# The conditional layer with its weights standing in the array and its result turned by DMA, and the last pair's base product undivided

## The chip, the cores and the metric

The kernel runs on one core of one Trainium2 chip. The metric is the device time of one execution in microseconds (us). A core has a matrix engine (PE, with its weight loads shown apart as PEld), a vector engine (DVE), a scalar engine (ACT), a pool engine (POOL) and a sync engine (SP) that issues most of the DMAs. Each engine works through its own queue in order: an instruction that waits holds everything behind it on that engine.

## What is computed

The input `x` is 64 samples of 64 channels by 1024 features. A block with a residual is followed by another one:

```python
y  = einsum('bct,bcd->bdt', x, cond_weights[itok_0_15])      # conditional layer: a 64 x 64 matrix for each sample
qkv = y.reshape(8, 8*64, 1024) ... @ qkvw + qkvb              # attention over 64 tokens, 32 heads of 32
x1 = x + softmax(q k / sqrt(32)) v @ ow + ob
base   = x1 @ W.T                                             # second conditional layer: base product and
logits = x1 @ Wr.T + language bias; top 2; softmax            #   two of eight low-rank experts
z  = bf16(base + 2 * sum(gate * (x1 @ A.T) @ B))
out = x1 + ffn(z)        # int8-like quantization, gate and up products, silu, clip, quantization, down product
```

All products but those of the feed-forward part are in float32, which the matrix engine takes in two instructions for each product of the program.

## The kernel before

**Stages.** The 4096 token rows are eight blocks of 512. `attention` (line 183) computes the conditional layer, q, k and v, scores, softmax and context, block by block. `OutProjection` (line 1069) multiplies by `ow` and adds the residual, for pairs of 256 rows. `second_stage` (line 1188) does the base product, the router, the experts and the feed-forward part, also by pairs. The large products (q, k, v, `ow`, `W`) are done as seven products of quarters (class `Winograd`, line 1009): with the token quarters `B11`, `B12`, `B21`, `B22` (features by tokens) and sums of them, `T1` to `T4`.

**The conditional layer.** A tile is two samples, 128 rows by 1024 features. `conditional` (line 342) copies the two 64 x 64 matrices of a tile into the diagonal of a 128 x 128 tile `wbd` (line 380), and multiplies eight 128 x 128 pieces of `x` as standing weights with `wbd` as moving data (line 355). So the result leaves the array already turned, features by tokens. Copies on DVE and ACT (lines 361, 363) put it into the token quarters `yB`, and four DVE instructions (line 376) form the sums `T`. This is eight pieces of work for each block; those of block b + 1 stand in the last phase of block b, ahead of its v and q, k products.

**The order in a block.** A block has four phases, c = 0 to 3 (`NP`), each for a quarter of the columns of q and k. During phase c the PE does the q and k products for c + 1 (`rows_job`, line 423); in phase 0 also the second half of v, in phase 3 the first half of v and the first q and k of the next block (`values_job`, line 456). In each phase two groups are begun (`group`, line 585), each with its score products (line 498, tile `s`), at the start and in the middle. When two groups have their probabilities turned, their context products (line 550, tile `c`) come right after the scores of a group. The order is planned by hand: `run` (line 615) adds up the costs that the author gave to the pieces in a clock `now`, and `at` files a step under the time when it is to be put into its engine's queue. A group's steps are: DVE takes the maximum and the difference, ACT the exponential (line 514), DVE normalizes, ACT parts the float32 numbers into two planes of 16-bit halves (line 528, tile `ph`, 6.8 planned us after the scores), SP turns them with a DMA transpose (line 533, tile `phT`), and 8 us later ACT joins the planes (line 540, tile `pT`).

**What a k job leaves.** The seven products come in the order 1, 6, 7, 5, 2, 4, 3. Product 2 is copied by four ACT instructions (line 419) into `kbd`, the block-diagonal keys, which have one buffer only; the others are added by DVE (line 421). The scores of the next phase read `kbd`, and so must wait for these copies.

**Loads.** `load_qk` (line 285) loads the seven combined quarters of q's or k's weights, 1792 KB, through SP at the end of the job that frees one of two buffers. In block 0 they are loaded raw and summed by the engines. `load_x` (line 239) loads the four tiles of the next block's `x`, 512 KB each, at the start of a block; POOL gathers the matrices `wg` by indirect DMA.

**The end.** The last pair p = 15 has an order written out by hand (lines 1554 to 1632), interleaved with the rest of pairs 14 (`q`) and 13 (`r`): `base` is one of seven products of four pieces, `after` its sums on DVE or ACT, `lora` the experts' product, `quant_a` and `quant_b` the quantization (by DVE and ACT) and the turning of its result (by DMA, or by the PE where the last argument is True), `gate_or_up`, `scaled`, `glu`, `down` and `result` the feed-forward part.

Of the kernel before, what the change touches and what calls it, by code (L numbers as in the profile page):

```python
# [11 lines left out]
F32 = mybir.dt.float32  # L12
# [170 lines left out]
def attention(tc, a, x_t, ctx_d, ident, dram, ps_g, KC, PB, NBLK, NCH, HPC, H, C, chores, early, op):  # L183
# [27 lines left out]
    with ExitStack() as ctx, ExitStack() as mid:  # L211
# [13 lines left out]
        w = pool(early, "w1", 1)  # L225
        xp = pool(early, "xp", 4)

# [10 lines left out]

        def load_x(b):
            tiles = []  # L240
            for j in range(PB):
                i = b * PB + j
                xt = xp.tile([P, H], F32, tag="x", name=f"x_{i}")
                if i == PB - 1:
                    held(xt[:, 0:1], tiles[0][0])
                nc.sync.dma_start(xt, x_t[i])
                wg = xp.tile([P, C], F32, tag="wg", name=f"wg_{i}")
                nc.gpsimd.indirect_dma_start(
                    out=wg[:, :],
                    out_offset=None,  # L250
                    in_=cw,
                    in_offset=bass.IndirectOffsetOnAxis(ap=idx[:, i:i + 1], axis=0),
                )
                tiles.append((xt, wg))
            return tiles

# [28 lines left out]
        def load_qk(b, wh, c, eng=None):  # L285
            t = w_qk[b, wh, c] = wp.tile([P, 7, KQ, P], F32, tag="wqk", name=f"w{wh}_{b}_{c}")
            if b == 0:
                if (wh, c) == ("q", 0):
                    held(t[:, SLOT["A11"], 0, 0:1], x_next[0][1])
                for key in RAW:  # L290
                    nc.sync.dma_start(t[:, SLOT[key], :, :], quarter(key, (0 if wh == "q" else H) + c * P, P))
                return sums(
                    eng or nc.vector, lambda key: t[:, SLOT[key], :, :], lambda: nc.gpsimd.dma_start(qk_d[wh, c], t)
                )
            nc.sync.dma_start(t, qk_d[wh, c])
# [20 lines left out]
        bqkv = act.tile([P, 3 * KC], F32, tag="bqkv", name="bqkv")  # L316
        x_next = load_x(0)
        first_sums = load_qk(0, "q", 0) + load_qk(0, "k", 0, nc.gpsimd)
# [5 lines left out]

        wbd = []
        for j in range(PB):
            t = w.tile([P, P], F32, tag=f"wbd{j}", name=f"wbd{j}")
            nc.vector.memset(t, 0.0)
            wbd.append(t)
        kbd, vbd = [], []  # L330
# [10 lines left out]

        def conditional(b, tiles):

            def one(hf, j):
# [3 lines left out]
                def product():  # L348
                    xt = tiles[j][0]
                    if j % 2 == 0:  # L350
                        B[key] = yp.tile([P, KQ, HB], F32, tag=key, name=f"y{key}_{b}")
                    ps = ps_g.tile([P, 4, P], F32, tag="g", name=f"cond_{b}_{j}_{hf}")
                    for q in range(KQ):
                        k = hf * KQ + q
                        nc.tensor.matmul(ps[:, q, :], xt[:, k * P:(k + 1) * P], wbd[j], start=True, stop=True)
                    box.append(ps)

                def rest():
                    dst = B[key][:, :, (j % 2) * P:(j % 2 + 1) * P]
                    if j % 2 == 0:  # L360
                        nc.vector.tensor_copy(dst, box[0])
                    else:
                        nc.scalar.copy(dst, box[0])  # L363
                    if (hf, j) == (0, 3):
                        t_of("T1", "B12", "B11")
                    elif (hf, j) == (1, 3):
                        t_of("T2", "B22", "T1")
                        t_of("T3", "B22", "B12")
                    elif (hf, j) == (1, 1):
                        B["T4"] = B["B12"]  # L370
                        nc.vector.tensor_tensor(B["T4"], B["B21"], B["T2"], ALU.subtract)
                return 0.95, product, rest

            def t_of(key, x, y):
                B[key] = yp.tile([P, KQ, HB], F32, tag=key, name=f"{key}_{b}")
                nc.vector.tensor_tensor(B[key], B[x], B[y], ALU.subtract)

            for j, (_, wg) in enumerate(tiles):
                for r in range(2):
                    (nc.gpsimd if b else nc.vector).tensor_copy(wbd[j][halves[r], halves[r]], wg[halves[r], :])  # L380
            return [one(0, j) for j in range(PB)] + [one(1, j) for j in (2, 3, 0, 1)]

# [197 lines left out]
        def contexts(least=1):  # L580
            ready = sum(len(pTs) == 2 for *_, pTs in waiting)
            for n in range(ready if ready >= least else 0):
                context(*waiting.pop(0), 1.7 * n * (least - 1))

        def group(b, c, us):


            def begin():
                ps = scores(b, c, us)
                if behind:  # L590
                    behind.pop()()
                contexts(2)
                pTs = []
# [85 lines left out]

        for f in conditional(0, x_next):  # L680
            run(*f)
# [4 lines left out]
        for f in qk_fill(0, 0) + v_fill(0, 0):  # L686
            run(*f)
        for b in range(NBLK):
            if b + 1 < NBLK:
                x_next = load_x(b + 1)  # L690
            for c in range(NP):
                fills, length = [], None
                if c + 1 < NP:
                    fills += qk_fill(b, c + 1)
                    if c == 0:
                        fills[7:7] = v_fill(b, 1)
                        if b == 0:
                            for at_ in range(3, 7):
                                with_sums(fills, at_, v_raw, 1)
                elif b + 1 < NBLK:  # L700

                    fills += conditional(b + 1, x_next) + v_fill(b + 1, 0) + qk_fill(b + 1, 0)
                else:
# [484 lines left out]
def second_stage(tc, a, out_t, xT_d, ident, ps_g, KC, NT, H, C, half, comb, op):  # L1188
# [12 lines left out]
    with ExitStack() as ctx:  # L1201
# [165 lines left out]
        def base(p, i):  # L1367
# [10 lines left out]
            elif i == 3:  # L1378
                lora(p, ps, 1, bmd)

        def lora_5(p):
            lora(p, st[p]["ps", 5], 1, bm[:, hs[1]])
# [22 lines left out]
        def quant_a(p, t, nm, between=None):  # L1405
# [11 lines left out]
            nc.vector.tensor_reduce(am, q, AX.X, ALU.max, apply_absolute_value=True)  # L1417
            sc = s["sc", nm, t] = sm.tile([P, 1], F32, tag="sc" + nm, name=f"sc_{nm}_{p}_{t}")
            nc.vector.tensor_scalar(sc, am, 1.0 / QMAX, 1e-8, ALU.mult, ALU.max)
# [52 lines left out]
        def down(p, t):  # L1472
            s = st[p]
            qT = s.pop(("qT", "i", t))
            for n in range(2):
                ps = s["pd", t, n] = ps_h.tile([P, HH], F32, tag="h", name=f"pd_{p}_{t}_{n}")
                for k in range(IC):
# [3 lines left out]

        def result(p, t, adds=None):
            s = st[p]
            y = p2.tile([P, H], F32, tag="y", name=f"y_{p}_{t}")
            si = s.pop(("sc", "i", t))
            for n in range(2):
# [3 lines left out]
                if adds:  # L1490
                    adds.tensor_add(y[:, hs[n]], y[:, hs[n]], s["x", t][:, hs[n]])
                    nc.sync.dma_start(out_t[2 * p + t, :, hs[n]], y[:, hs[n]])
# [10 lines left out]
        for p in range(NPAIR - 1):  # L1503
# [17 lines left out]
            do(old, quant_b, q, 0, "u")  # L1521
            base(p, 7)
            do(last, down, r, 1)
            do(last, result, r, 1)
# [40 lines left out]
        down(r, 0)  # L1565
        token_sums(p)
        quant_a(r, 1, "i")
        base(p, 1)
        after(p, 1)
        route(p)  # L1570
        quant_b(r, 1, "i")
        result(r, 0)
        base(p, 6)
        base(p, 7)
        gates_transposed(p)
        after(p, 6)
        quant_a(q, 0, "u")
        base(p, 2)
        after(p, 2)
        after(p, 7)  # L1580
        quant_a(q, 1, "g", (q, 0, "u"))
        down(r, 1)
        result(r, 1)
        quant_a(q, 1, "u", (q, 1, "g"))
        gate_or_up(q, 0, "g")
        scaled(q, 0, "g")
        base(p, 4)
        after(p, 4)
        gate_or_up(q, 0, "u")
        quant_a(p, 0, "g", (q, 1, "u"))  # L1590
        scaled(q, 0, "u")
        base(p, 5)
        lora_5(p)
        after(p, 5)
        quant_a(p, 0, "u", (p, 0, "g"))
        glu(q, 0)
        gate_or_up(q, 1, "g")
        quant_b(p, 0, "u")
        base(p, 3)
        scaled(q, 1, "g")  # L1600
        after(p, 3)
        gate_or_up(q, 1, "u")
        quant_a(p, 1, "g")
        gate_or_up(p, 0, "g")
        scaled(q, 1, "u")
        quant_a(p, 1, "u", (p, 1, "g"))
        gate_or_up(p, 0, "u")
        quant_a(q, 0, "i")
        glu(q, 1)
        quant_b(p, 1, "u", True)  # L1610
        gate_or_up(p, 1, "g")
        quant_a(q, 1, "i", (q, 0, "i"))
        gate_or_up(p, 1, "u")
        down(q, 0)
        scaled(p, 0, "g")
        scaled(p, 0, "u")
        quant_b(q, 1, "i")
        glu(p, 0)
        scaled(p, 1, "g")
        scaled(p, 1, "u")  # L1620
        result(q, 0)
        quant_a(p, 0, "i")
        down(q, 1)
        glu(p, 1)
        quant_b(p, 0, "i", True)
        result(q, 1, nc.gpsimd)
        quant_a(p, 1, "i")
        down(p, 0)
        result(p, 0, nc.gpsimd)
        quant_b(p, 1, "i", True)  # L1630
        down(p, 1)
# [55 lines left out]
```

## Time and profile before

| what | value |
|---|---|
| median of 3 runs | 2462.17 us (2460.88 to 2463.17) |
| the profiled execution's own time | 2461.01 us |
| its span in the profile | 2459.1 us |
| PE, DVE, ACT, POOL busy | 99%, 62%, 39%, 15% of the span |
| DMA queues q1 (SP), q0, q10 | 52.9%, 7.7%, 2.0% of 16 engines |
| granted PE clock | 0.995 of full |

The profile is of one execution, recorded by the hardware. Times are us from the start of the span, unless marked ns. A row of groups gives line, engine, operation, the tile written <- the tiles read, the shape, the count, then the busy time in us and the mean ns of one, and after the second bar the engine's idle time ahead of them with what ended it. A row of the timeline gives start, duration, engine, line and operation; in brackets the idle time before it and its releaser. A matmul's row shows two instructions for each float32 product, and the duration of each overlaps with the next: the distance from one row's start to the next one's is the time it takes. The DMA rows give the median us from issue to landing.

### The profile page before, as it was taken

Reading aid. Unit: us, or ns where it says so; the run is one execution under the profiler, and the core shown is the slowest. Engines: PE = TensorE matmul, PEld = TensorE weight load, DVE = VectorE, ACT = ScalarE, POOL = GpSimd, SP = SyncE. Lnnn points to the kernel's source line nnn. Section 1 sums busy time; section 2 is a strip of 40 time slices with the busy share of each in tenths; the row PEclk is TensorE's granted clock in tenths of the full one; section 3 lists DMA queues with packets and bytes.
Section 4 is the critical chain, followed back from the end, with each engine's and each line's share of the span. In section 5 each row is a group of like instructions: output and inputs, shape, how many; then the busy total and the mean of one; then the engine's idle time right before and its main releaser. Section 6 shows DMA issues by size and latency. Waiting matters only on the chain.

```text
span 2459.1 us, 34200 instructions
## 1 busy us (share of the span) xinstructions
PE 2423.2 (99%) x13194; PEld 1699.6 (69%) x13232; DVE 1533.1 (62%) x2957; ACT 952.8 (39%) x1303; POOL 363.4 (15%) x451
## 2 busy tenths in 40 slices
PE   8999999999999999999999999999999999999996
PEld 7888888888888888888888544444454545454452
DVE  4685585775664755745646623333367777778787
ACT  1353353342443533534424544344323333333333
POOL 5110001011122221210000233333200000000001
PEclk9999999999999999999999999999999999999998
DMA  8895767676677767775547588876744344434343
GB/s 280 284 264 152 219 200 238 188 208 210 201 198 250 206 194 246 207 208 175 177 137 234 170 258 255 263 243 215 242 126 83 84 79 88 80 81 87 70 95 72
DMA packets 417980, 446.76 MB, mean 182 GB/s; under 512 B 299665, under 2 KB 353938, under 8 KB 404114
## 3 DMA queue, kind: packets, MB, share of 16 engines
q1 hardware_dynamic: 387298, 377.90, 52.9%
q0 software_dynamic: 12080, 49.82, 7.7%
q10 hardware_dynamic: 18432, 16.79, 2.0%
q8 instruction: 106, 1.74, 0.3%
q14 instruction: 64, 0.52, 0.1%
HBM read 272.97 MB, written 100.66 MB: 152 GB/s over the span
## 4 chain that ended last, share of the span: by engine, by line
PE 94%; DVE 2%; ACT 2%; DMA 1%; issue 0%; ACTq 0%; SPq 0%; DVEq 0%
PE psva L462 5%; PE pska L435 5%; PE psvd L462 5%; PE psqa L435 5%; PE psvc L462 4%; PE pbc L1031 4%; PE pba L1031 4%; PE psqc L435 4%; PE pskc L435 4%; PE psqd L435 4%; PE pskd L435 4%; PE pbd L1031 4%; PE poa L1031 4%; PE pod L1031 4%; PE poc L1031 4%; PE s L498 3%
## 5 line engine op out<-in xcount | busy, mean ns | idle before, releaser
L540 ACT COPY pT<-phT 128x1024 int16<-128x1024 int16 x128 | 167.2, 1342 | 84.8 <-DMA phT<-ph 84.6
L514 ACT ACTIVATE prob<-prob 128x512 f32<-128x512 f32 x128 | 80.6, 630 | 259.4 <-DVE prob L511 232.1
L421 DVE SCALAR_TENSOR_TENSOR kbd<-pskd,bqkv,psku 32x256 f32<-32x256 f32 x256 | 123.1, 481 | 31.6 <-PE pskd L435 27.8
L528 ACT COPY ph<-prob 128x1024 int16<-128x1024 int16 x128 | 130.8, 1047 | 24.3 <-DVE prob L522 23.7
L1152 POOL TENSOR_TENSOR xo<-xo,ob 128x1024 f32<-128x1024 f32 x32 | 84.1, 2648 | 351.7 <-DVE To L1042 305.5
L561 ACT ACTIVATE co<-c,bqkv 128x256 f32<-128x256 f32 x128 | 60.1, 469 | 179.6 <-PE c L550 152.1
L435 PE MATMUL psqa<-yB,wq 128*128 128x256 f32 x512 | 123.6, 384 | 0.5 <-ACT psqp L406 0.5
L435 PE MATMUL pska<-yB,wk 128*128 128x256 f32 x512 | 122.6, 382 | 0.0
L1495 POOL DMA_DIRECT2D out_dram<-y x29 | 25.2, 869 | 652.3 <-DVE y L1487 652.3
L1126 ACT COPY xh<-xo 128x1024 int16<-128x1024 int16 x64 | 64.1, 1040 | 142.4 <-DVE xo L1171 142.4
L462 PE MATMUL psva<-wv,yB 128*128 128x256 f32 x512 | 117.0, 382 | 0.4
L1031 PE MATMUL poa<-woA,cx 128*128 128x512 f32 x256 | 115.4, 593 | 0.0
L1031 PE MATMUL pba<-wtA,x1T 128*128 128x512 f32 x256 | 115.1, 592 | 0.0
L1137 ACT COPY xTo<-xhT 128x1024 int16<-128x1024 int16 x64 | 84.7, 1339 | 58.4 <-DMA xhT<-xh 52.1
L435 PEld LDWEIGHTS pska<-yB,wk 128*128 128x128 f32 x512 | 96.0, 190 | 15.0 <-issue 2.6
L435 PEld LDWEIGHTS psqa<-yB,wq 128*128 128x128 f32 x512 | 95.2, 190 | 16.0 <-issue 2.8
L462 PEld LDWEIGHTS psva<-wv,yB 128*128 128x128 f32 x512 | 96.1, 190 | 14.1 <-ACT yB L363 1.0
L510 DVE TENSOR_REDUCE mx<-s 128x8 f32<-128x512 f32 x128 | 87.7, 685 | 10.7 <-PE s L498 9.3
L511 DVE TENSOR_TENSOR prob<-s,mx 128x512 f32<-128x512 f32 x128 | 88.5, 691 | 9.3 <-DVE mx L510 0.5
L522 DVE TENSOR_TENSOR prob<-prob,den 128x512 f32<-128x512 f32 x128 | 88.5, 692 | 4.4
L520 DVE TENSOR_REDUCE den<-prob 128x8 f32<-128x512 f32 x128 | 86.7, 678 | 7.2 <-ACT prob L514 6.3
L1031 PEld LDWEIGHTS poa<-woA,cx 128*128 128x128 f32 x256 | 48.4, 190 | 60.1 <-issue 59.9
(243 smaller groups left out, 5135.5 us busy)
## 6 DMA issues: line engine op xcount, KB each, us to landing
wv<-v_d SPq DMA_DIRECT2D x98, 512.0 KB, 3.9
wq<-q_d SPq DMA_DIRECT2D x28, 1792.0 KB, 7.7
wk<-k_d SPq DMA_DIRECT2D x28, 1792.0 KB, 8.1
x<-in_x_dram SPq DMA_DIRECT2D x32, 512.0 KB, 9.1
ctx_d<-co ACTq DMA_DIRECT2D x128, 128.0 KB, 4.2
cx<-ctx_d SPq DMA_DIRECT2D x16, 1024.0 KB, 6.9
xo<-in_x_dram SPq DMA_DIRECT2D x32, 512.0 KB, 5.7
xT_d<-xTo SPq DMA_DIRECT2D x64, 256.0 KB, 3.2
```

The lines of the kernel that those rows point to most:

```text
L421: nc.vector.scalar_tensor_tensor(dst, ps, bias, u, ALU.add, ALU.add)
L435: nc.tensor.matmul(ps[:, 0:HB], A[:, SLOT[A_OF[i]], k, :], B[B_OF[i]][:, k, :], start=first and k == 0, stop=k == KQ - 1, skip_group_check ...
L462: nc.tensor.matmul(ps[:, j * VC:(j + 1) * VC], B[B_OF[i]][:, k, j * P:(j + 1) * P], A[:, k, :], start=first and j == 0 and k == 0, stop=k ...
L510: nc.vector.tensor_reduce(mx_v, ps, AX.X, ALU.max)
L511: nc.vector.tensor_tensor(p.rearrange("p (a e) k -> p a e k", a=2), ps, mx_v.unsqueeze(3).to_broadcast([P, 2, HPC, C]), ALU.subtract)
L520: nc.vector.tensor_reduce(den, p, AX.X, ALU.add)
L522: nc.vector.tensor_tensor(p, p, den.unsqueeze(2).to_broadcast([P, n, C]), ALU.mult)
L528: nc.scalar.copy(h, planes(p.rearrange("p n k -> p (n k)")))
L540: nc.scalar.copy(planes(pT.rearrange("p a b q -> p (a b q)")), hT)
L1031: self.nc.tensor.matmul(ps, self.B[self.B_OF[i]][:, k, :], self.A[self.A_OF[i]][:, k, :], start=first and k == 0, stop=k == self.KQ - 1, s ...
L1137: nc.scalar.copy(planes(xT.rearrange("p k q -> p (k q)")), hT)
L1152: nc.gpsimd.tensor_add(s["x"][:, t, :], s["x"][:, t, :], self.ob)
```

## The change

The conditional layer of blocks 1 to 7 is turned round. `wg` itself stands in the array, in quarters of 64 x 64, and `x` moves: four products of 64 rows by 512 columns for a tile, one for each quarter of the array, into two tiles of the pool `ps_c`, which the context products use too. The result is tokens by features, so it is parted into 16-bit planes by ACT (`yh`, a pool with one buffer), turned by a DMA transpose through SP (`yhT`, two buffers) and joined by ACT into the token quarters, which now have two sets, for even and odd blocks. That is for each tile two transposes and five ACT instructions. The tiles stand singly in the order: at the start of those groups that have no context products, and once in phase 0 between jobs. The sums `T` of the next block stand in the last two products of phase 2 and the first two of phase 3. `x` has two buffers instead of four, and a tile's load is issued when the tile two before it has been multiplied. Block 0 keeps the old way, with its tiles lent from the quarters.

For the last pair the base product is not done in seven products but in four, one for each half of the tokens and half of the columns, of eight pieces each (`undivided`), with the raw quarter `A21` of the weights loaded for it in the iteration before. The sums of tokens and the sums after the products fall away, and the order of the last pairs is written anew.

```diff
-        xp = pool(early, "xp", 4)
+        xp = pool(early, "xp", 2)
...
-        wbd = []
-        for j in range(PB):
-            t = w.tile([P, P], F32, tag=f"wbd{j}", name=f"wbd{j}")
-            nc.vector.memset(t, 0.0)
-            wbd.append(t)
+        wbd = yp.tile([P, KC, P], F32, tag="B21", name="wbd")
+        nc.vector.memset(wbd, 0.0)
...
+        def conditional_tile(b, j):
+            xt, wg = x_of.pop((b, j))
+            ps = [ps_c.tile([P, 2, HB], F32, tag="c", name=f"cond{hf}_{b}_{j}") for hf in range(2)]
+            for hf in range(2):
+                for r in range(2):
+                    nc.tensor.matmul(
+                        ps[hf][halves[r ^ hf], :, :], wg[halves[r], :], xt[halves[r], hf * 512:(hf + 1) * 512],
+                        start=True, stop=True,
+                    )
+            if j + 2 < PB:
+                load_x(b, j + 2)
+            elif b + 1 < NBLK:
+                load_x(b + 1, j + 2 - PB)
+            def parted_y(hf):
+                h = w.tile([P, 2, 512], I16, tag="yh", name=f"yh_{b}_{j}_{hf}")
+                nc.scalar.copy(h, planes(ps[hf].rearrange("p a t -> p (a t)")))
+                at(now + 1.7, lambda: turned_y(hf, h))
+            def turned_y(hf, h):
+                hT = w.tile([P, 2, 512], I16, tag="yhT", name=f"yhT_{b}_{j}_{hf}", bufs=2)
+                nc.sync.dma_start(
+                    hT.rearrange("p h (k q) -> p (h k) q", q=P), h.rearrange("p h t -> p (h t)"), transpose=True
+                )
+                at(now + 5.1, lambda: joined_y(hf, hT))
+            def joined_y(hf, hT):
...
+                for r in range(2) if hf else (slice(0, P),):
...
+                    nc.scalar.copy(dst, src[:, :, :, halves[r] if hf else r])
+            at(now + 1.7, lambda: parted_y(0))
+            at(now + 5.1, lambda: parted_y(1))
...
-                contexts(2)
+                if not contexts(2) and (b, c, us[0]) != (0, 0, 0):
+                    next_tile()
...
+                        n = 7 if b else 14
+                        fills[n:n] = [(0.9, next_tile, None)]
+                    if c + 2 == NP and b + 1 < NBLK:
+                        sums_to_come = [lambda b=b, n=n, Y=Y: t_of(b + 1, Y, *T_OF[n]) for n in range(4)]
+                        with_sums(fills, -2, sums_to_come, 1)
+                        with_sums(fills, -1, sums_to_come, 1)
...
-                    fills += conditional(b + 1, x_next) + v_fill(b + 1, 0) + qk_fill(b + 1, 0)
+                    fills += v_fill(b + 1, 0) + qk_fill(b + 1, 0)
+                    with_sums(fills, 0, sums_to_come, 1)
+                    with_sums(fills, 1, sums_to_come, 1)
...
+        def undivided(p, t, n):
...
+            ps = s["ps", t, n] = ps_g.tile([P, HH], F32, tag="g", name=f"pb{t}{n}_{p}")
+            for h in range(2):
+                for k in range(KQ):
+                    nc.tensor.matmul(
+                        ps, s["xT"][:, t, h * KQ + k, :], AT[f"A{n + 1}{h + 1}"][:, k, :],
+                        start=(h == 0 and k == 0), stop=(h == 1 and k == KQ - 1), skip_group_check=True,
+                    )
+        def completed(p, t, n):
+            lora(p, st[p]["ps", t, n], t, bm[:, hs[n]])
+        def rounded(p, t, n):
+            s = st[p]
+            nc.scalar.copy(s["z"][:, t, hs[n]], s.pop(("ps", t, n)))
...
+            if p == NPAIR - 2:
+                AT["A21"] = wa.tile([P, KQ, HH], F32, tag="wtS3", name="wtA21")
+                nc.sync.dma_start(AT["A21"], quarters(a["w_t"])[:, 0, :, 1, :])
```

In the new order of the last pairs the four `undivided` products stand where the seven `base` products stood, a `quant_a` of 1024 columns is split in halves for the last tile (`quant_half`, `quant_whole`), the last `down` products use the pool `ps_g`, the quantized up input of the last tile is turned by DMA and no longer by the PE, and one of the two last additions to the result of tile 0 moves from POOL to DVE.

## The prediction

> **What bounds the kernel now.** I read the page first. These are its busy times and the row of the PE in 40 slices:
>
> ```profile
> PE 2423.2 (99%) x13194; PEld 1699.6 (69%) x13232; DVE 1533.1 (62%) x2957; ACT 952.8 (39%) x1303; POOL 363.4 (15%) x451
> PE   8999999999999999999999999999999999999996
> ```
>
> The PE is the bound everywhere but in the last slice. So an edit wins what PE time it takes out, and loses what PE wait it puts in. Next, the group of the old conditional products, and where they stand in one block (timeline of the PE):
>
> ```profile
> L355 PE MATMUL cond<-wbd,x 128*128 128x128 f32 x512 | 61.7, 282 | 10.2 <-DVE wbd L380 9.5 <-DVE yB L361 0.7
> ```
>
> ```profile
> 350.57 7.41 PE L355 MATMUL cond<-wbd,x 128*128 128x128 f32 x64
> 357.82 3.62 PE L462 MATMUL psva<-wv,yB 128*128 128x256 f32 x16
> ...
> 475.65 1.10 PE L498 MATMUL s<-kbd,qT 64*64 64x128 f32 x32
> 476.69 1.99 PE L435 MATMUL pska<-yB,wk 128*128 128x256 f32 x8
> ...
> 488.97 1.10 PE L498 MATMUL s<-kbd,qT 64*64 64x128 f32 x32
> ```
>
> Start to start, a block's conditional layer takes 7.25 us, a group's scores 1.04 us, and the second half of phase 1 (block 2) 13.32 us. ACT in that half:
>
> ```profile
> 478.35 0.63 ACT L514 ACTIVATE prob<-prob 128x512 f32<-128x512 f32 x1 [5.57 <-DVE prob L511]
> 479.74 0.63 ACT L514 ACTIVATE prob<-prob 128x512 f32<-128x512 f32 x1 [0.76 <-DVE prob L511]
> 480.27 0.35 ACT L406 COPY pskp<-pska 128x256 f32<-128x256 f32 x1
> 480.53 2.55 ACT L540 COPY pT<-phT 128x1024 int16<-128x1024 int16 x2
> 482.93 1.99 ACT L528 COPY ph<-prob 128x1024 int16<-128x1024 int16 x2
> 485.62 1.92 ACT L419 ACTIVATE kbd<-pska,bqkv 32x256 f32<-32x256 f32 x4 [0.70 <-PE pska L435]
> ```
>
> The last row is what counts: `kbd` is ready at 487.54, and the scores that read it start at 488.97. The slack is 1.43 us, although ACT is idle more than half of the time on average. Then the DMA issues of three short stretches: the start of block 1, a quiet stretch of phase 1, and the load of the q weights at 475.75.
>
> ```profile
> x<-in_x_dram SPq DMA_DIRECT2D x4, 512.0 KB, 9.1
> wk<-k_d SPq DMA_DIRECT2D x1, 1792.0 KB, 7.0
> ...
> phT<-ph SPq DMA_TRANSPOSE x2, 6.0
> ```
>
> ```profile
> phT<-ph SPq DMA_TRANSPOSE x2, 3.2
> ```
>
> ```profile
> wq<-q_d SPq DMA_DIRECT2D x1, 1792.0 KB, 9.4
> ```
>
> A transpose lands after 3.2 us in the quiet stretch, and after 6.0 where loads were issued on SP's queue ahead of it: what is issued later comes later. Last, the tail of the PE:
>
> ```profile
> 2429.48 1.03 PE L1439 MATMUL qTp_u<-ident_b,qb_u 128*128 128x128 bf16 x8 [7.18 <-DVE qb_u L1432]
> 2430.31 3.41 PE L1449 MATMUL pg<-wg,qT_g 128*128 128x512 bf16 x8
> 2433.55 1.89 PE L1449 MATMUL pu<-wu,qT_u 128*128 128x512 bf16 x8
> ```
>
> **Conditional products.** A new tile is four products of 64 rows and 512 columns, two instructions each. The nearest row is the scores: sixteen products of 128 columns on the same four quarters of the array in 1.04 us. Four of 512 move as many columns, so a tile costs 1.03, and a block 4 x 1.03 = 4.12. Saved: 7.25 - 4.12 = 3.13 us in each of seven blocks, 21.9, and 0.7 for the wait on `yB` in the group row. Here a rule speaks against the change. The Trainium skill (TensorEngine Tiling (Array Packing), Gotcha 1: PSUM Pressure) says that different row tiles must not use one PSUM bank at once. The scores keep to it (each half of the rows writes its own bank); a new tile does not, since both halves of the rows write into both banks. If the halves then take turns, a tile costs about 1.9 us, 28 tiles 53, and the gain of 22.6 is gone. I take the row, 1.03, as nothing shows that the two writes at different partitions collide, and keep 1.9 for the range.
>
> **What the tiles put on ACT and SP.** For each tile ACT gets two partings (row L528: 1.0 each), one joining of 1.3 (L540) and two halves of it at 0.7, 4.7 us in all, and SP two transposes. On average ACT has room. But the parting of the second half needs the one buffer `yh`, which is free only when the transpose of the first half has landed. That transpose is put in 1.7 planned us before the parting, and needs 3.0 us at the least (tile `phT`: 3.0/3.5/7.5 from issue to landing). So ACT stands still at each tile, and everything behind it on ACT with it: one `pT`, the partings of the probabilities, the first joining, and the copies to `kbd`, for which the next scores, hence the PE, wait.
>
> I walk through the half shown above, where tile 3 of the block stands. Times count from the start of its scores, S. PE: scores 1.03, tile 1.03, seven products 7 x 1.727; the next scores are due at S + 14.2. SP: the load of wq is issued at S + 0.1 and lands at S + 9.5, as before; behind it the `x` tile (512 KB; that stretch of block 1 moved 318 GB/s, so 1.6 us) and the first transpose (about 1.4 once it starts): it lands at S + 12. ACT: the exponentials, the first parting, the copy of product 1 and one `pT` are done at S + 7.3; then 4.7 us of standing still. From S + 12: parting 1.05, `pT` 1.27, two partings 2.0, joining 1.3, four copies to `kbd` 1.92, which gives S + 19.6. **The PE waits 5.4 us** at the scores of phase 2. Where tile 2 or tile 1 falls into a q or v job, nothing on the PE waits (next bank needed some 3 us later), though ACT is behind and costs 0.7 at the next block's start.
>
> Sum over blocks: 5 x 5.4 = 27 in blocks 1 to 5; 4.1 in block 6, which has no `x` to load; in block 0, where the tiles come one group later, 4.4 (tile 2, behind raw quarters of wq) and 2.4 (tile 1 in the k job, no load ahead): together 38; 0.7 at five starts, 3.5. In all 41.4. From both sides: if the transpose landed in its quiet 3.2 us, ACT's own work would just reach and the wait would be 0 to 0.3; if the load lasts 1 us longer, it is 6.4.
>
> The clock, too. After 7.18 idle us eight gate products took 3.24 us (2430.31 to 2433.55) and not 1.73. The Trainium skill (TensorE: Matmul & The Clock Gate, What's actually happening) lets the clock fall to half after an idle window of 3.4 us, windows running freely. By the trace's row alone (7.18 us) a wait of 5.4 may cost nothing or 1.5; by the rule it holds a whole window 6 times in 10. I take 0.7 for six blocks: 4.
>
> **Edits at nothing.** The removed copies on DVE (28 x 0.68) and POOL (56 x 0.28) lay under PE work. The sums `T` move into the k job of phase 2, where DVE is busy 11 of 13 us; each stands a product ahead of its use, so 0 (up to 1.2 a block if not). `x` loads are spread, 20 us ahead of use. SP's later probability transposes slip by ACT's delay, but their readers come 8 us later and the context products later still. The memset of `wbd` lies in DVE's wait for `wg` at the start. `A21`, 1 MB, lands in some 10 us, some 50 ahead of its use; what SP holds behind it is not due sooner.
>
> **The tail.** Undivided: 32 pieces instead of 28, 4 x 0.86 = 3.4 us more on the PE. Gone from DVE: four sums of tokens (4 x 0.65) and five sums after products (5 x 0.69), 6.0; added: halves instead of wholes and one addition, 1.5. From 2376 on the PE is idle for 13.5 us in six gaps (7.18 + 2.80 + 1.99 + 0.68 + 0.68 + 0.16), and DVE sets the pace (9.2 of 10 us from 2420 to 2430). Walking both orders through with these durations, the old one ends its last addition at 2452.6 (trace: 2454.0) and the new one at 2448.9: 3.7 less, and 0.8 as no gap of 7 us is left to slow the clock: 4.5. Bounds: 0 and 7.
>
> **Sum**, against the profiled execution of 2461.0 (span 2459.1 and 1.9 around it; the median of the runs is 1.2 higher): -22.6 + 41.4 + 4 - 4.5 = +18.3, so 2479.3, and **2480** as a median.
>
> **Rivals.** (a) *The queue does not hold the transpose up.* If its packets pass the wq load, it lands 4.7 us or more sooner, `kbd` is late by 0.3 us at most, and what remains is -22.6 - 4.5 + 7 x 0.5 + 1 = -22.6: 2439, or a little less. It decides from a wait under (22.6 + 4.5)/7 = 3.9 us a block. For it: many transposes land at 3.0 to 3.5. Against: 6.0 in the loaded stretch, and the very load ahead of it took 9.4. (b) *The bank rule bites*: 28 x 0.87 = 24 more, of which part hides in the wait for `kbd`, as ACT gains the same time: about 2495. Against: nothing measured; for: the rule. (c) *Gain and wait cancel*: waits of 3.5 to 4.5 a block, no change to be measured: 2462.
>
> **How the numbers follow.** Forecast 0.63, own range 2468 to 2494; (a) 0.20; (b) 0.11; (c) 0.06. Measurement tells 0.2% (4.9 us) from no change. Slower: the forecast and (b), 0.74. Same: (c), 0.06. Faster: (a), 0.20. The range runs from 2438 to 2500: it leaves out about half of (a), 0.10, and some of (b) and of long waits, 0.08.
>
> **What would show it.** Right: scores rows at each phase 2 with 4 to 7 us of idle ended by ACT `kbd`, the second `yh` parting waiting on the DMA `yhT`, tile products of 1.03 us. Wrong: `yhT` landing in under 4 us in the second half of phase 1; scores starting on time; tiles of 1.9 us; a tail, from the last router products to the end, that is shorter by less than 2 us.

## The result, and the profile after

The changed kernel takes 2523.6 us (median of 5 runs, 2516.5 to 2524.8), the kernel before 2461.9 on the same chip: a ratio of 1.0246, 95% interval 1.0234 to 1.0257, or +61.7 us. The prediction said +18.

The page of the kernel after, its busy times and the group of the new copies `yh`:

```profile
PE 2426.4 (96%) x12970; PEld 1671.0 (66%) x13008; DVE 1510.0 (60%) x2924; ACT 1054.9 (42%) x1416; POOL 349.3 (14%) x394
L407 ACT COPY yh<-cond 128x1024 int16<-128x1024 int16 x56 | 56.6, 1010 | 185.4 <-DMA yhT<-yh 184.8 <-PE cond L396 0.2
```

The PE has fewer instructions and yet is busy 3 us longer, and no longer 99% of the time. ACT stood still for 184.8 us before the new copies. Three rows of what the PE waits for (waits view: total, times, longest), none of them in the kernel before:

```profile
PE s L552 <- ACT kbd L473: 39.0, 16, 7.8
PE c L604 <- ACT yh L407: 11.7, 3, 7.1
PE cond L396 <- ACT yh L407: 4.8, 1, 4.8
```

The first row is the wait that the prediction named. The other two it had excluded ("nothing on the PE waits"). In the stretch that it walked through (second half of phase 1, block 2, S = 493.66), first SP, then ACT, then the PE:

```profile
485.06 7.06 SPq L412 DMA_TRANSPOSE yhT<-yh  x2
...
495.83 0.52 SPq L294 DMA_DIRECT2D wq<-q_d  x1
```

```profile
496.89 1.00 ACT L407 COPY yh<-cond 128x1024 int16<-128x1024 int16 x1
...
508.80 1.01 ACT L407 COPY yh<-cond 128x1024 int16<-128x1024 int16 x1 [8.88 <-DMA yhT<-yh]
...
513.98 1.90 ACT L473 ACTIVATE kbd<-pska,bqkv 32x256 f32<-32x256 f32 x4
```

```profile
494.59 1.04 PE L396 MATMUL cond<-x,wg 64*64 64x512 f32 x8
...
514.96 0.68 PE L552 MATMUL s<-kbd,qT 64*64 64x128 f32 x2 [6.46 <-ACT kbd L473]
515.93 1.12 PE L552 MATMUL s<-kbd,qT 64*64 64x128 f32 x14 [0.29 <-ACT kbd L473]
516.99 3.37 PE L604 MATMUL c<-pT,vbd 128*64 128x64 f32 x64
```

The tile costs 0.97 us from start to start (its row 1.04), where 1.03 was forecast. The load of `wq` is issued at S + 2.2 and not at S + 0.1, because SP was still behind with the tile before: its two transposes take up 7.06 us in the queue, as the second waits for the second parting; the second parting starts at S + 15.1 and not at S + 12, `kbd` is ready at S + 22.2 and not at S + 19.6, and the PE waits 6.75 us. The contexts then take 3.37 us; they take 2.08 at full clock. The granted clock in that stretch (windows; the third number from the right is the PE's clock):

```profile
500.00:508.00 8.00, 8.00 (x41) 6.79 (x43) 6.67 (x14) 0.00 (x0) 0.00 (x0) 1.00 0.85 234
514.00:517.00 3.00, 1.75 (x18) 1.02 (x18) 0.00 (x0) 2.92 (x7) 0.47 (x1) 0.50 1.13 266
517.00:520.00 3.00, 3.00 (x61) 3.00 (x60) 2.67 (x4) 0.88 (x3) 0.69 (x2) 0.52 0.84 325
```

The other place is the second half of phase 0. In block 3, SP, then ACT, then the PE:

```profile
620.64 0.44 SPq L137 DMA_DIRECT2D seen_d<-seen  x1
631.02 0.29 SPq L139 DMA_DIRECT2D row<-seen_d  x1
...
631.86 1.24 SPq L412 DMA_TRANSPOSE yhT<-yh  x1
```

```profile
638.74 1.01 ACT L407 COPY yh<-cond 128x1024 int16<-128x1024 int16 x1 [16.69 <-DMA yhT<-yh]
```

```profile
639.80 2.36 PE L604 MATMUL c<-pT,vbd 128*64 128x64 f32 x32 [7.13 <-ACT yh L407]
```

The first half of a tile was parted at 617.89, but its transpose came into SP's queue behind two weight loads and two small DMAs (`seen_d` and `row`), the second of which waits for the first and was issued 10.4 us after it. So the second parting started 21 us after the first. All that time the tile held a PSUM buffer of `ps_c`, and half of the contexts found none.

**Where the 55.5 us of the two profiled executions are.** Up to the start of block 7 (first scores at 1261.5 before, 1319.3 after) the PE's idle time grows from 2.1 to 57.1 us: +55.0. The clock costs 19.3 us (summed over windows of 5 us: one minus the granted clock, times the PE's busy time; before 0.0). The two make 74.3, the stretch grew by 57.8, so 16.5 us of the gain from the products are seen. From there to the end it is 2.4 us shorter (1197.7 and 1195.3).

### The profile page after: what moved, and what is told of

The parts are those of the page before. It is cut to its first block, busy times and chain, and to the rows that moved or that the text cites. A ratio compares the mean times of both kernels' runs of the same rounds, so it can differ in the third digit from the quotient of the medians.

```text
span 2514.6 us, 33929 instructions
## 1 busy us (share of the span) xinstructions
PE 2426.4 (96%) x12970; PEld 1671.0 (66%) x13008; DVE 1510.0 (60%) x2924; ACT 1054.9 (42%) x1416; POOL 349.3 (14%) x394
## 4 chain that ended last, share of the span: by engine, by line
PE 85%; DMA 7%; ACT 5%; DVE 2%; issue 1%; SPq 0%; ACTq 0%; DVEq 0%
DMA yhT<-yh 5%; PE psva L516 5%; PE psqa L489 4%; PE pbc L1102 4%; PE pbd L1102 4%; PE pba L1102 4%; PE psvc L516 4%; PE poa L1102 4%; PE pod L1102 4%; PE poc L1102 4%; PE psqd L489 4%; PE psqc L489 4%; PE psvd L516 4%; PE pska L489 3%; PE pskc L489 3%; PE pskd L489 3%
## 5 line engine op out<-in xcount | busy, mean ns | idle before, releaser
L407 ACT COPY yh<-cond 128x1024 int16<-128x1024 int16 x56 | 56.6, 1010 | 185.4 <-DMA yhT<-yh 184.8
L516 PE MATMUL psva<-wv,yB 128*128 128x256 f32 x512 | 122.3, 393 | 0.0
L552 PE MATMUL s<-kbd,qT 64*64 64x128 f32 x2048 | 81.0, 283 | 39.1 <-ACT kbd L473 39.0
L574 DVE TENSOR_REDUCE den<-prob 128x8 f32<-128x512 f32 x128 | 86.7, 677 | 40.6 <-ACT prob L568 40.5
L1102 PE MATMUL pba<-wtA,x1T 128*128 128x512 f32 x240 | 107.9, 592 | 0.0
L552 PEld LDWEIGHTS s<-kbd,qT 64*64 64x64 f32 x2048 | 59.4, 136 | 65.9 <-ACT kbd L473 44.2
```

The lines of the kernel that those rows point to most:

```text
L516: nc.tensor.matmul(ps[:, j * VC:(j + 1) * VC], B[B_OF[i]][:, k, j * P:(j + 1) * P], A[:, k, :], start=first and j == 0 and k == 0, stop=k ...
L552: nc.tensor.matmul(ps[halves[r], hp, n, jj * 2:(jj + 1) * 2, :], q_of[b, c][halves[hp], m, t * HB + t0:t * HB + t0 + C], kbd[u][halves[hp] ...
L574: nc.vector.tensor_reduce(den, p, AX.X, ALU.add)
L1102: self.nc.tensor.matmul(ps, self.B[self.B_OF[i]][:, k, :], self.A[self.A_OF[i]][:, k, :], start=first and k == 0, stop=k == self.KQ - 1, s ...
```

## The experiments

Times are medians, the difference is to the kernel before on the same chip, the ratio has its 95% interval. "After" is +61.7.

**The two halves of the change.** The attention of after with the tail of before, and the reverse.

> The conditional part alone: tiles on standing weights and turned by DMA in the attention, and the tail of the kernel before. Theory A (all of the loss lies in the attention, and the undivided tail gives a little back): 2526 us, 2 to 5 more than the whole change. Rival (the tail costs, or hands a loss on through the clock or the queues): 2523 or less.

> The attention of before with the undivided product of the last pair. The prediction gave it 4.5 us, 2457.5. Theory A: the trace of after shows 2.3 us less from the start of block 7 to the end, so 2459.5. Rival (the tail is worth what the prediction said, and after lost the rest of it to something that the conditional layer left behind): 2457.5 or less. A tail that costs would show as 2463 or more.

Conditional part alone: 2530.1, +69.1 (1.0286, 1.0272 to 1.0300). Tail alone: 2456.6, -4.4 (0.9983, 0.9976 to 0.9990). The tail wins what the prediction gave it, 4.5, and not the 2.3 that I had expected from one pair of traces. All of the loss lies in the attention.

**A second buffer for `yh`.** It needs 2 KB for each partition. In the first two kernels they come from `co`, in the third from the chores of GpSimd:

```diff
-  h = w.tile([P, 2, 512], I16, tag="yh", ...)
+  h = w.tile([P, 2, 512], I16, tag="yh", ..., bufs=2)
   # yh2, yh2_late:  cop = pool(ctx, "co1", 3, ...), wg of the first block's last tiles in "B22"
   # yh2_late also:  at(now + 10, lambda: joined_y(hf, hT))
   # two_yh:         b = st.tile(..., tag="b", ..., bufs=1), co and wg as in after
```

> Two buffers for yh instead of one (room from one buffer less of co, and the wg of the first block's last two tiles in a quarter that stands free). Theory A (the single buffer makes ACT stand still, and all that is late follows from it): the second parting waits for nothing, ACT's 185 us of waiting for yhT falls under 40, the scores of phase 2 start within 2 us of before, and the time is 2437 to 2450. Rival B (the DMA queue itself is what is late: loads behind transposes, transposes behind loads, whoever waits for them): the first joining takes the wait over, and the time stays over 2480.

> Two buffers for yh, and the joining of a turned half put in 10 planned us after its transpose and not 5.1, so that ACT meets it only after it has landed. Theory A: no wait of ACT for yhT is left, 2435 to 2442, and a little under two buffers alone if the first joining still stood still there. Rival B: over 2480, as the loads behind the transposes are late all the same.

> Two buffers for yh again, but with the room for the second taken from the GpSimd chores (one buffer for their tile b instead of two), so that co keeps its four and wg stays as it was. Theory A (the single yh is the whole loss; what stayed in the run before with three co buffers, 12 us in block 0 and some 2 at each phase 2, was ACT waiting for co): 2434 us, 2431 to 2440: 22.6 less for the products and 4.4 for the tail. Rival (those 2 us a block come from the transposes and loads in the queue): 2450 to 2466.

yh2: 2466.4, +5.4 (1.0026, 1.0017 to 1.0034). yh2_late: 2465.0, +4.0 (1.0019, 1.0011 to 1.0026). Neither theory had these: in yh2 the wait of ACT for `yhT` fell to 40, but ACT waited 71 us for the DMA that empties `co` instead, a side effect of my own edit. With the room from elsewhere, two_yh: 2443.5, **-19.6 (0.9917, 0.9903 to 0.9930)**, 81 us under after, from one buffer of 2 KB. What is left in two_yh of the waits (PE, then ACT):

```profile
PE s L552 <- ACT kbd L473: 4.4, 6, 1.9
```

```profile
ACT yB L426 <- DMA yhT<-yh: 34.2, 21, 6.9
```

It still misses the 2434 of theory A by 9.5, and lies 3.5 above its range. The rival had 2450 or more. Blocks 1 and 6 there take 166.7 us, 3.4 and 3.9 less than before; block 0 takes 2.2 more, where 3 less was due, and block 3 is 3 over its due.

**When ACT comes to the second parting.** Same copies and DMAs, only the planned time of the second parting is later: for all tiles, or for the second of each block.

```diff
-  at(now + 5.1, lambda: parted_y(1))
+  at(now + 11, lambda: parted_y(1))                         # late_all
+  at(now + (11 if j == 1 else 5.1), lambda: parted_y(1))    # late_one
```

> One yh buffer as in after, but the second parting put in 11 planned us after the product and not 5.1, so that the transpose of the first half has landed when ACT comes to it. The same copies, the same DMAs. Theory A (ACT standing still is the loss): 2434 to 2446. Rival (the loss is the amount of work on ACT and the queue ahead of kbd): the kbd copies are as late as before, 2490 or more. A second rival: the tile holds both ps_c buffers longer, and contexts wait for them: 2450 to 2480.

> As after, but only the tile in the v job of phase 0 (the second of each block) has its second parting 11 planned us after the product. Theory A: the 28 us that the second half of phase 0 took longer in after (contexts waiting for the PSUM buffers that this tile holds) go, the waits of phase 2 stay: 2495 us, 2488 to 2501. Rival (that stretch is late because SP's queue is): over 2512.

late_all: 2523.4, +60.4 (1.0254, 1.0235 to 1.0272). late_one: 2522.7, +59.7 (1.0243, 1.0227 to 1.0259). Both missed: theory A as I had put it falls. The rivals' figures (2490 or more, over 2512) came true, but in late_all not for the rival's reason: the wait for `kbd`, which it had as long as before, fell from 39.0 to 11.6. A later plan does not help where the transpose lands later still (in block 3 of late_one the second parting waited 14.6 us even so). In late_all the one buffer is taken for longer, and the next tile's first parting finds it full (14 times, 135 us on ACT): a new wait of the PE of 20.5 us for the copies of product 1. What is short is the buffer's time, from a parting to the landing of its transpose, twice in each tile.

**What is ahead of the transposes.** The `x` load put behind them; the weight load on ACT's queue; four sevenths of the `wq` load put behind them; the chores' flag on GpSimd's queue.

```diff
-  load_x(b, j + 2)
+  at(now + 8.5, lambda: load_x(b, j + 2))                   # x_late (both branches)
-  nc.sync.dma_start(t, qk_d[wh, c])
+  nc.scalar.dma_start(t, qk_d[wh, c])                       # loads_act
+  n = 3 if (wh, c) == ("q", NP - 1) else 7                  # split_load
+  nc.sync.dma_start(t[:, 0:n], qk_d[wh, c][:, 0:n])
+  if n < 7:
+      at(now + 10.5, lambda: nc.sync.dma_start(t[:, n:7], qk_d[wh, c][:, n:7]))
-  nc.sync.dma_start(seen_d, seen)                           # flag_pool (row as well)
+  nc.gpsimd.dma_start(seen_d, seen)
```

> As after, but each x tile is loaded 8.5 planned us later, behind the transposes of its tile and not ahead of them. The prediction put the x load in front of the transpose at 1.6 us. If so, with the clock's share, six waits at phase 2 are 1.6 to 2.5 us shorter each and phase 0 gains some as well: 2508 to 2516. Rival (the x load costs the transpose nothing, it is the wq load alone that holds it): 2520 to 2526.

> As after, with one yh, but from block 1 on the q and k weights are loaded from ACT's DMA queue and not from SP's, so that no transpose stands behind 1.8 MB of weights in its queue, while the bytes that move at the time stay the same. Theory A (order within the queue makes the transposes late): they land in some 4 us, the waits for kbd at phase 2 go for the most part, 2470 to 2490; what is left is the second half of phase 0, where wv loads and the flag of the chores stand ahead. Rival (the 16 DMA engines are shared, whatever the queue): landing as late as before, over 2510.

> As after, one yh, but the load of the q weights that starts with the second half of phase 1 is split: three of its seven parts at the old time, the other four some 9 us later, behind the transposes of that tile. The same bytes in all, 1 MB less ahead of the first transpose. Theory A (the bytes that are on the way ahead of a transpose set when it lands): it lands about 5 us sooner in blocks 1 to 5, the waits for kbd there go nearly, with their clock: 5 x 7, 2489 (2482 to 2500). Rival (SP being held, or the amount of ACT's work, makes kbd late): over 2512.

> As after, but the two small DMAs of the chores' flag (out and back in, once, in block 3) are issued from GpSimd's queue. In after SP stood 11 us at the second of them, and the transposes of that block's second tile behind it. Theory A: block 3 falls from 188 us to about 178, no other block changes, 2514 (2509 to 2518). Rival (that tile is late for another reason): no change, 2520 to 2526.

x_late: 2503.5, +40.5 (1.0159, 1.0144 to 1.0175): 21 us for 0.5 MB moved, more than either theory had. split_load: 2505.1, +40.9 (1.0163, 1.0147 to 1.0178), between the two. loads_act: 2554.8, +93.8 (1.0359, 1.0331 to 1.0387), worse than after. In block 2 the transpose issued at 536.3, with `wq` on the other queue since 531.2 and `x` ahead of it in its own, landed at 545.2: 8.8 us, where after has 10.8 and theory A had some 4. In block 0 another one, issued at 177.2 with `wq` on ACT's queue 1.6 us behind it, landed at 203.3 (3.0 us after its issue in after), and with ACT the PE stood still, for 20.7 us:

```profile
203.33 1.38 ACT L426 COPY yB<-yhT 128x512 int16<-128x512 int16 x2 [21.48 <-DMA yhT<-yh]
```

Block 0 takes 204.4 us there and 182.2 in after: 22 of the 40 us between the two traces. So another queue did not bring the transposes sooner. The Trainium skill (DMA: Bandwidth & Descriptors, Queues, rings and completion order) has the queues of SP and ACT on the same 16 engines, taking turns by packets, which agrees with the 8.8 us; why the other one took 26.1 is not shown. The kernel also put load waits into ACT's order, and what part of the rest is due to that is not shown either.

flag_pool: 2520.6, +56.4 (1.0224, 1.0209 to 1.0240); the second half of phase 0 in block 3 lost 5 of its 10.5 us over, but the whole cannot be told from after.

Why split_load gave half is seen in block 4 (S = 854.3). SP first, then ACT:

```profile
858.35 0.92 SPq L295 DMA_DIRECT2D wq<-q_d  x1
```

```profile
865.89 1.01 ACT L410 COPY yh<-cond 128x1024 int16<-128x1024 int16 x1 [4.81 <-DMA yhT<-yh]
```

The shortened load went out 4.0 us late, held by the tile before, and so the parting still started at S + 11.6. That led to the last pair of runs.

**What a wait costs the clock.** The kernel before, with copies on ACT ahead of the `kbd` copies that nobody reads:

```diff
+  if 0 < b < NBLK - 1 and (c, us[0]) == (1, 2):
+      at(now + 8.6, lambda: [nc.scalar.copy(idle[:, 1, :], idle[:, 0, :]) for _ in range(5)])   # or 9
```

> The kernel before, with five copies on ACT that nobody reads (128x1024 int16, 1.0 us each), put ahead of the kbd copies of the second half of phase 1, in blocks 1 to 6. Slack of 1.4 and 0.7 idle on ACT ahead of kbd leaves a PE wait of 2.9 us, six times: 17. If a short wait costs the clock nothing: 2478. If it costs the clock 1.5 to 2.5 us each, as the longer waits of after seem to: 2487 to 2493.

> The same with nine copies: a PE wait of 6.9 us, six times, 41. If the clock costs 0.7 for each wait, as the prediction had it: 2506. If it costs 2 to 3 us each: 2514 to 2520.

copies5: 2482.0, +21.1 (1.0088, 1.0073 to 1.0104). copies9: 2512.4, +51.5 (1.0216, 1.0200 to 1.0231). The waits were 2.0 and 6.0 us each (11.8 and 36.1 in all), a little under what I expected. By the windows the clock cost 4.4 us in copies5 and 13.7 in copies9: 0.7 and 2.3 for each wait. In copies5 it cost three of the six blocks some 1.5 us and the others nothing; one that it hit:

```profile
493.16 0.43 PE L500 MATMUL s<-kbd,qT 64*64 64x128 f32 x2 [1.43 <-ACT kbd L421]
494.13 1.13 PE L500 MATMUL s<-kbd,qT 64*64 64x128 f32 x14 [0.54 <-ACT kbd L421]
495.19 3.01 PE L552 MATMUL c<-pT,vbd 128*64 128x64 f32 x64
```

Why three of six, when the breaks are alike, can be read from the clock of all 20 traces. Every change of it lies, in each trace, on a grid of 3.41 us. Of the 14,213 windows of this grid that ran at full clock (the first 15 and the last 4 us of a trace left out), all 148 in which the PE was busy for 1.50 us or less (by the profile) were followed by half clock, 4 of the 35 between that and 1.72, and none of the 14,030 above. So a whole idle window is not needed, only one that is less than about half busy, and where the grid cuts a short break decides. The windows of the break in blocks 4 and 6 of copies5, each with the one after it (busy time of the PE in front, its clock third from the right):

```profile
838.61:842.02 3.41, 1.44 (x32) 0.79 (x26) 1.93 (x5) 2.57 (x5) 2.45 (x5) 1.00 0.96 273
842.02:845.43 3.41, 3.41 (x65) 3.29 (x63) 2.66 (x4) 0.95 (x2) 0.00 (x0) 0.50 0.96 359
1186.77:1190.18 3.41, 1.94 (x23) 1.07 (x21) 3.08 (x7) 3.33 (x6) 0.00 (x0) 1.00 0.48 125
1190.18:1193.60 3.42, 2.93 (x80) 2.67 (x81) 2.00 (x4) 1.17 (x3) 0.00 (x0) 1.00 0.96 407
```

**Which tiles.** Two buffers for the first three tiles of a block and one for the last (the tile that the prediction walked through), and the reverse:

```diff
+  tag="yh2" if hf and j < 3 else "yh"     # last_single
+  tag="yh2" if hf and j == 3 else "yh"    # last_double
```

> Two yh buffers for the first three tiles of each block, one for the last, which is the tile that the prediction walked through. If the walk was right for its own tile (a PE wait of 5.4 us, with 2.3 for the clock as the run with nine copies showed) and went wrong only in what the other tiles hand on: 5 x 7.7 and some 5 for block 6 over the 2443 of two buffers, 2487 (2480 to 2492). If that tile alone makes the waits as long as in after (9 us over in blocks 1 to 5): 2494 to 2500.

> The other way round: two yh buffers for the last tile of each block alone, one for the first three. The prediction's step that nothing on the PE waits where these fall into q and v jobs would give 2443 to 2446. What the trace of after shows in the second half of phase 0 (28 us over all blocks) would give 2471, and some us more where their delay is handed on to the next scores: 2470 to 2485.

last_single: 2478.3, +13.9 (1.0053, 1.0036 to 1.0070), a little under the expected range. last_double: 2497.0, +32.7 (1.0139, 1.0122 to 1.0155), well over it. Against two_yh the last tile's single buffer costs 33.5 us and the other three's 52.3, together 86, where after is 81 over: the two add up, nearly. Block 1 of last_single (S = 313.9), SP, ACT, PE:

```profile
314.02 0.33 SPq L294 DMA_DIRECT2D wq<-q_d  x1
```

```profile
325.25 1.01 ACT L407 COPY yh<-cond 128x1024 int16<-128x1024 int16 x1 [5.07 <-DMA yhT<-yh]
```

```profile
331.42 0.68 PE L552 MATMUL s<-kbd,qT 64*64 64x128 f32 x2 [2.65 <-ACT kbd L473]
332.39 1.12 PE L552 MATMUL s<-kbd,qT 64*64 64x128 f32 x14 [0.29 <-ACT kbd L473]
```

Here the walk holds: `wq` at S + 0.1 as it said, ACT idle 5.07 us (4.7), the second parting at S + 11.3 (12), `kbd` ready at S + 18.4 (19.6); only the PE waits less, 2.9 us (5.4). Over blocks 1 to 5 the load goes out 0.3 us after S on average, and the PE waits 3.2 us for `kbd`; in after it is 3.2 and 6.7; in last_double 3.1 and 2.3, though its last tile has both buffers. The delay of one tile comes to the next through SP's queue.

**For a best version.** On two_yh: the later `x` loads; the flag on GpSimd's queue; that, and the two half joinings of each tile on GpSimd.

```diff
+  (nc.gpsimd.tensor_copy if hf else nc.scalar.copy)(dst, src[...])     # two_yh_pool
```

> Two yh buffers and the later x loads together. If ACT standing still is the loss and the queue only sets how long it lasts, two buffers alone have left little for the x loads: the first joining's waits and the rest in blocks 0 and 3, 2434 to 2441 against 2443 with two buffers alone. Rival (what x_late won, 20 us, was the queue's own cost): 2425 or less.

> Two yh buffers and the flag from GpSimd's queue: a try for the best version. Block 3, 169.7 us with two buffers alone, falls to 167: 2441 (2438 to 2444). Rival: 2443 to 2446, as before.

> As the try for the best version, with the two half joinings of each tile on GpSimd, which is idle 85% of the time, and not on ACT. If ACT's work ahead of kbd is what is left in blocks 0 and 4: 2435 to 2439. If GpSimd is slow at them, or holds DVE up: 2442 or more.

two_yh_x: 2446.7, -14.2 (0.9943, 0.9930 to 0.9957). two_yh_flag: 2444.7, -19.5 (0.9919, 0.9906 to 0.9933). two_yh_pool: 2442.6, -21.6 (0.9911, 0.9896 to 0.9926). The first lies above both of its expectations, the other two where their rivals had them. None is better than two buffers alone by more than the runs tell, and x_late's 21 us do not come again: they were only the length of a wait that is no longer there.

## Why the prediction was off

- **Direction and mechanism** were right: one `yh`, ACT standing still, `kbd` late. Rival (a), a transpose that passes the load, is out by the waits; rival (b), the bank rule, by the tile row of 1.04 us; rival (c), a gain and a wait that cancel, by the measured time.
- **The step that failed**: "Where tile 2 or tile 1 falls into a q or v job, nothing on the PE waits". I compared one bank's due time with ACT's delay, and did not follow what else a late tile holds. It holds its PSUM buffers, so that contexts and a tile product waited 16.5 us. And it holds SP, so that the next load, and with it the next tile, is late. In the terms of its sum: the last tile was put at 31.1 (27 and 4.1) and up to 4 for the clock, and costs 33.5 (near by luck, as the clock's bullet shows); the other three were put at 10.3 (6.8 in block 0 and five starts of 0.7), and cost 52 by last_double (the clock's share is in both). These 42 us are nearly all of the difference between +18 and +61.7.
- **The wait for `kbd`** was put at 5 x 5.4, 4.1, and 6.8 in block 0: 37.9. The trace shows 39.0, but not for the reason given. The tile alone makes 20.0 (last_single), since half of the scores start without the late keys and `kbd` comes 1.2 us sooner than walked (S + 18.4); the rest is handed on by the tiles before. A slip of the walk: its terms for the transpose (9.5, 1.6 and 1.4) add up to S + 12.5, where it says 12.
- **The clock** was put at 0.7 for each of six waits, 4. It cost 19.3. I took the trace's one row, 7.18 us of idle time, as near the threshold. The Trainium skill (TensorE: Matmul & The Clock Gate, What's actually happening), weighed in the prediction, lets the clock halve after one idle window of some 3.4 us, windows running freely: 6 waits in 10. The grid of 3.41 us agrees; the idle window does not, as a window busy for 1.44 us was enough in copies5 (a break of 2.4 us from the end of the first scores, with 0.43 us of products in it), and the measurement decides. By it each wait of 5.4 us halves the clock, as the grid leaves at least 2.7 us of it in one window; the waits of 6.0 us in copies9 did so in six blocks of six, at 2.3 us each. In last_single the clock's 13.2 us make good the idle time that I had put too high, so that its +13.9 comes near the +18 of the prediction: two errors that cancel.
- **The products**: 3.13 a block predicted; the undisturbed blocks 1 and 6 of two_yh give 3.4 and 3.9. Right. In after only 16.5 of the 22 are seen; the other 5 I could not place in idle or clock.
- **The tail**: 4.5 predicted, 4.4 by itself. Right. That the trace of after shows only 2.4 from block 7 on is two things. From the last router products (their rows stand below, before and after) to the end it takes 82.5 us before and 78.4 after, 4.1 less; but from the start of block 7 up to them it takes 1115.1 and 1116.8, 1.7 more. In x_late these are 79.7 and 1121.0. So the tail won what it should, and part of that was lost again ahead of it, which no run takes apart.

```profile
2376.60 3.87 PE L1300 MATMUL pr<-awr,x1T 128*128 128x136 f32 x32
2436.19 3.87 PE L1371 MATMUL pr<-awr,x1T 128*128 128x136 f32 x32
```

- **Edits at nothing**: no run takes them one by one, but blocks 1 and 6 of two_yh, which won more than their due, leave no room for a cost. What failed is the order on SP's queue: "what SP holds behind it is not due sooner" was asked for `A21` alone, not for the tile transposes behind loads and the flag.

Still open: what is left in two_yh against its due (in its trace 5 us in block 0, 3 in block 3, and some 4 from block 7 on), and 18 of the 40 us by which the trace of loads_act is over that of after.

## What to carry to other kernels

When a buffer is filled by one engine and emptied by a DMA, its time runs from the write to the landing (for `yh` in after 5.3 us at the median and up to 20.8); count how often it is needed in that time before giving it a single copy, and follow a late one through everything that it holds: its PSUM buffers, and the queue that issues the next loads. A wait in one place of a periodic schedule is walked through with the delay that the place before hands on, not from a clean start. Add the clock to each PE wait of more than some 2 us: here 0.7 us for 2.0 and 2.3 for 6.0. An estimate from the windows above (busy 1.50 of 3.41 us or less always halved it, over 1.72 never): a wait of 3.8 us or more is always hit, one under 1.7 never by itself, and between them it is chance.

## What the hardware showed that was not expected

- The clock changed only on a grid of 3.41 us, and halved after windows that were less than about half busy: after 2.0 us of waiting in three blocks of six (some 1.5 us lost each). It came back only after a window in which the PE was busy for 2.7 us or more, so the half clock lasted 3.41, 6.83 or 10.24 us in after.
- Products of different rows of the array, writing one PSUM bank at different partitions, took 1.04 us for four times 512 columns, as long as scores whose halves write different banks: no turn-taking. The rule on banks that the prediction weighed did not show as time here.
- Transposes took 3.0 us from issue to landing at the least and 4.3 at the median, but up to 10.8 with loads of 1.8 MB and 0.5 MB ahead, 8.8 with the larger load on another queue, and 26.1 at the worst there (loads_act).
